# A four-layer graph network on one core: work by half periods, norm and degree roots as powers on GpSimd, and the adjacency scaled once

## The chip, the core and the metric

The kernel runs on one core of a Trainium2 chip. The metric is the device time of one execution in microseconds. The core's engines are TensorE (PE, with its weight loads shown apart as PEld), VectorE (DVE), ScalarE (ACT), GpSimd (POOL) and SyncE (SP, which here only issues DMAs). Each engine works through its own queue in order and waits on semaphores for the others.

## What is computed

There are 64 graphs of 256 nodes with 128 features, and a 256 x 256 adjacency of zeros and ones for each. Four layers follow one another; each adds its result to its input and normalizes the rows (a layernorm without weights):

```python
# layer 0: the largest relu(p_i + q_j + b) over the neighbours j of i
h = jax.nn.relu(p[:, :, None, :] + q[:, None, :, :] + b) * adj[..., None]
x = LN(x + jnp.max(h, axis=2))
# layer 1: sums over neighbours, in both directions, of elu projections, then tanh
upd = jnp.concatenate([adj @ in_rep, node_rep, adj.T @ out_rep], axis=2)
x = LN(x + jnp.tanh(upd @ W_upd.T + b_upd))
# layer 2: two graph convolutions with the normalized adjacency
A_hat = adj + I;  dinv = rsqrt(A_hat.sum(-1));  norm_A = dinv_i * A_hat * dinv_j
h = elu(elu(x @ W0 + b0)); h = elu(norm_A @ (h @ W1) + b1); x = LN(x + norm_A @ (h @ W2) + b2)
# layer 3: a message gelu(LN(m_j + m_i + b1)) for every edge, summed over j, and an update
agg = sum_j adj_ij * gelu(LN(m_j + m_i + b1) * g1 + be1)
x = LN(x + LN(concat(x, agg) @ W2 + b2) * g2 + be2)
```

## The kernel before

A graph's 256 nodes lie as two halves of 128 (h = 0, 1), one row to a partition. Since a node has some 10% to 15% of the others as neighbours, layers 0 and 3 do not form all pairs. Every node's neighbours are counted off into 40 slots; nodes are sorted by degree (the matrix perm), so that slot s is used by a prefix of them, and the prefixes add up to WIDTH = 4800 columns for each half of the neighbours. A 0/1 matrix hot (128 x 2 x 4800) says which neighbour stands in which column, and a product with it spreads the neighbours' features over the columns.

The work on a graph is cut into four generators, which yield now and then:

- `first` (L502): loads x and the adjacency, finds degrees and the sorted order (sign, L551; perm, L560), the ranks, and builds hot on DVE (L629, L635); then, from L645 on, layer 0: products with hot in tiles of 512 columns (L665), corrections for empty slots (L681), maxima on DVE (`fold`, L492), and the norm to x1. It takes 44 calls; the 17th ends with hot.
- `second` (L778, `layer_1`): layer 1, 14 calls. Its first steps are the transposed x1 (L207), the product L223 and the addition L226; its products with the adjacency are L238 and L240.
- `third` (L782, `layer_2`): the degrees' root, the unit matrix added to the adjacency in place (L277), then layer 2 with its two convolutions. Each scales the features by dinv (L293), multiplies them by the adjacency (L296) and the weights (L304), and scales by dinv again (L308). After that come layer 3's projections (c3, dT; L797, L810) and `sums_of` for the first four tiles. It takes 34 calls, of which 23 lead up to dT and 11 are the four `sums_of`.
- `last` (L821): `sums_of` for the remaining six tiles; for each of the ten tiles the product with the fetched scale (L839), Gelu (L841) and the sum over slots (`fold`); then the aggregation (L860) and the update (`update`) with two norms. It takes 34 calls; in its first 18 are five tiles' messages.

`sums_of` (L718) forms the pair sums of a tile of up to 1024 columns (product L728, addition L732), their squares (ACT, L736) and column sums (L743), and sends these through DRAM: line, then vr in a compact form, root and reciprocal there, then scale_line, which `last` fetches spread over all partitions (rs_s, L828). The tile pre that it fills has 7 buffers.

A norm is `layernorm` (L166 on): statistics on DVE, `rs` (L174), a yield, `inverse_root` (Sqrt on ACT, L74, then a reciprocal on DVE, L75), a yield, and the subtraction and scaling on DVE (L180, or L184 and L185). There are five norms to a graph, one root of degrees (dinv), and five roots of vr.

Four graphs are in work at once, one in each stage. `together` runs the generators of one step side by side: it always calls the one that has done the smallest share of its stated number of calls, the oldest stage first on a tie:

```python
STAGES = [(last, 34), (third, 34), (second, 14), (first, 44)]
...
for u in range(1 - len(STAGES), U):
    together(*[
        (n, part(g0 + u + i, ss[u + i])) for i, (part, n) in enumerate(STAGES) if 0 <= u + i < U
    ])
```

So there are 67 steps ("periods") for 64 graphs, of which the first three and the last three are not full. There is no barrier between the periods. The semaphores, the places of the tiles and the final order on each engine come from the tile framework when the kernel is built: it follows the order of the calls and moves some instructions forward (in the trace an addition of `sums_of`, L732, stands between L706 and L707, which `first` issues one after the other).

Of the kernel before, what the change touches and what calls it, by code (L numbers as in the profile page):

```python
# [9 lines left out]
F32 = mybir.dt.float32  # L10
BF16 = mybir.dt.bfloat16
AF = mybir.ActivationFunctionType
ALU = mybir.AluOpType
# [30 lines left out]
def kernel(  # L44
# [24 lines left out]
    minus1 = consts.tile([P, 1], F32, name="minus1")  # L69
    nc.vector.memset(minus1, -1.0)  # L70

    def inverse_root(t):

        nc.scalar.activation(t, t, AF.Sqrt)  # L74
        nc.vector.reciprocal(t, t)  # L75

    def load(src, shape, name):
        t = consts.tile(shape, F32, name=name)
# [78 lines left out]
    class Shared:  # L157
# [45 lines left out]
        def to_features(self, xn, name, bufs=None):  # L203
# [5 lines left out]
            nc.scalar.copy(t, pt[:, :N])  # L209
            return t  # L210

        def node_tile(self, name):
            return self.state.tile([P, H, P], F32, name=name)

# [43 lines left out]
            yield from self.layernorm(x2, y)  # L258
            s["x2"] = x2

        def layer_2(self, s, aT, deg_of):

            work, psum, elu = self.work, self.psum, self.elu
            x2 = s["x2"]
            deg = work.tile([P, H], F32, name="deg")
            deg_of(deg)
            nc.vector.tensor_scalar(deg, deg, 1.0, None, ALU.add)
            pos = work.tile([P, H], F32, name="pos")
            nc.vector.tensor_scalar(pos, deg, 0.0, None, ALU.is_gt)
            dinv = work.tile([P, H], F32, name="dinv")  # L270
            nc.vector.tensor_scalar(dinv, deg, 1e-30, None, ALU.max)
            inverse_root(dinv)
            yield
            nc.vector.tensor_mul(dinv, dinv, pos)
            for h in range(H):
                blk = aT[:, h, h * P:(h + 1) * P]
                nc.vector.tensor_add(blk, blk, ident)  # L277
            yield
            xT = self.to_features(x2, "xT_2", 1)
            yield  # L280
# [8 lines left out]
            yield from elu(hs, hs, twice=True)  # L289
            yield  # L290
            for step in (1, 2):
                for h in range(H):
                    nc.vector.tensor_scalar(hs[:, h], hs[:, h], dinv[:, h:h + 1], None, ALU.mult)  # L293
                pa = psum()
                for h in range(H):
                    nc.tensor.matmul(pa[:, :N], hs[:, h], aT[:, h], start=h == 0, stop=h == H - 1)  # L296
# [14 lines left out]
                if step == 1:  # L311
                    yield from elu(hs, hs)
                yield
# [26 lines left out]

    def together(*gens):

        gens = [[0, n, gen] for n, gen in gens]
        while gens:
            e = min(gens, key=lambda e: e[0] / e[1])
            e[0] += 1
            if next(e[2], gens) is gens:
                gens.remove(e)


# [3 lines left out]
    def sparse(ctx):  # L354
# [147 lines left out]
        def first(g, s):  # L502
# [37 lines left out]
            nc.scalar.activation(diff, diff, AF.Abs, accum_out=fl[:, 0:1])  # L540
            kc = work.tile([P, H, H], F32, name="kc")
            nc.vector.scalar_tensor_tensor(kc, pc, -1.0, down_c, ALU.mult, ALU.subtract)
            dg = state.tile([P, H], F32, name="dg", bufs=3)
            nc.vector.tensor_reduce(dg, pc, AX.X, ALU.add)
            s["dg"] = dg

            more = work.tile([P, H, H], F32, name="more")
            for h in range(H):
# [169 lines left out]
        def sums_of(s, i):  # L718
# [46 lines left out]
                fu[:rows],  # L765
                s["fulls"].rearrange("h w -> (h w)")[first_at:first_at + n].rearrange("(p k) -> p k", k=PIECE),
            )
            inverse_root(vr[:rows])
            nc.vector.tensor_mul(vr[:rows], vr[:rows], fu[:rows])
            out_line = dram.tile([1, GROUP * TILE], F32, name="scale_line")  # L770
            nc.sync.dma_start(out_line[:, :n].rearrange("o (p k) -> (o p) k", k=PIECE), vr[:rows])
# [9 lines left out]

        def third(g, s):  # L782

            dg = s["dg"]

            def deg_of(deg):
                nc.vector.tensor_scalar(deg, dg, 1.0 / N, None, ALU.mult)

            yield from sh.layer_2(s, s["aT"], deg_of)
            yield  # L790
            x3, perm = s["x3"], s["perm"]

# [83 lines left out]


        U = next(u for u in (UNROLL, 8, 4, 2, 1) if B % u == 0)
        STAGES = [(last, 34), (third, 34), (second, 14), (first, 44)]

        def steps(g0):
            ss = [{} for _ in range(U)]
            for u in range(1 - len(STAGES), U):
                together(*[
                    (n, part(g0 + u + i, ss[u + i])) for i, (part, n) in enumerate(STAGES) if 0 <= u + i < U
                ])

        if U == B:
            steps(0)
# [5 lines left out]
    def general(ctx):  # L895
# [82 lines left out]
        def middle(g, s):  # L978
# [7 lines left out]
                nc.scalar.copy(aT[:, hj], pt[:, :N])  # L986
            yield

            def deg_of(deg):
                nc.vector.tensor_reduce(deg, an, AX.X, ALU.add)  # L990

            yield from sh.layer_1(s, an, aT, s["x1"])
            yield
            yield from sh.layer_2(s, aT, deg_of)
            yield

            x3T = sh.to_features(s["x3"], "x3T")
# [80 lines left out]
        def run():  # L1078
            nc.vector.memset(ones3, 1.0)

            with tc.For_i(0, B, U) as g0:
                ss = [{} for _ in range(U)]

                def stage(part, u):
                    return [(1, part(g0 + u, ss[u]))] if u < U else []
# [57 lines left out]
```

## Time and profile before

| what | value |
|---|---|
| median of three runs | 5732.97 us (5730.31 to 5735.6) |
| the profiled execution's own time | 5731.62 us |
| its span, first to last instruction | 5729.7 us |
| instructions | 83531 |
| mean granted TensorE clock | 0.862 of full speed |
| HBM traffic | 345.07 MB read, 14.53 MB written; DMA engines busy about a fifth of the time |
| DVE: pre by rs_s, L839 | 732.9 us in 640 instructions |
| ACT: Gelu, L841 | 594.2 us in 512 instructions and 686.4 us in 535 table loads ahead of it |
| ACT: table loads ahead of Exp, L194 | 283.5 us in 221 |
| POOL | 10 instructions, all in the set-up |

"Busy" is time in which an engine worked on an instruction; the rest of its span it waited. A group in the profile is one line of the kernel on one engine, with the number of its instructions, their busy time, the mean length of one in ns, and the idle time of the engine just before them with what ended it.

### The profile page before, as it was taken

The numbers are of one execution on the slowest core, as the hardware profiler recorded it, in microseconds if no ns is written. First come the engines' busy times: TensorE is split into PE (matmuls) and PEld (weight loads), VectorE is DVE, ScalarE is ACT, GpSimd is POOL, SyncE is SP. The second block draws the span as 40 slices with busy tenths as digits, with TensorE's granted clock in tenths as the row PEclk, the third lists the DMA queues.
The fourth block names the chain that finished last, engine by engine and source line by source line (L and its number), as shares of the span: only waits on it lengthen the run. The fifth ranks groups of instructions, "written<-read, shape, count | busy, mean of one in ns | idle before, by whom it ended". The sixth has DMA issues, their size and how long they took to land.

```text
span 5729.7 us, 83531 instructions
## 1 busy us (share of the span) xinstructions
PE 4529.9 (79%) x27408; PEld 2508.7 (44%) x27408; DVE 4834.4 (84%) x14654; ACT 4275.2 (75%) x6485; POOL 1.9 (0%) x10
## 2 busy tenths in 40 slices
PE   5878878878778778788788788787887887877875
PEld 2444444444444444444444444444444444444443
DVE  6788888888888888888888888888888888888876
ACT  2577777777777777777777777777777777777785
POOL 0000000000000000000000000000000000000000
PEclk8888889889889889888898898898888887888986
DMA  0122222222212221221221222122212212221222
GB/s 22 44 70 63 62 63 72 62 63 66 69 57 70 65 63 63 72 63 62 63 72 62 63 65 70 59 68 65 63 62 72 64 62 63 69 66 60 68 65 74
DMA packets 292813, 365.15 MB, mean 64 GB/s; under 512 B 151952, under 2 KB 210448, under 8 KB 292368
## 3 DMA queue, kind: packets, MB, share of 16 engines
q1 hardware_dynamic: 292368, 359.73, 20.0%
q8 instruction: 217, 3.56, 0.3%
q14 instruction: 228, 1.87, 0.1%
HBM read 345.07 MB, written 14.53 MB: 63 GB/s over the span
## 4 chain that ended last, share of the span: by engine, by line
PE 52%; DVE 29%; ACT 11%; issue 4%; DMA 3%; SPq 0%; DVEq 0%; POOL 0%; ACTq 0%
PE bigp L665 11%; PE bigp L728 8%; DVE pre L839 6%; PE mm L860 5%; DVE lanes L492 4%; PE mm L743 4%; DVE hot L629 4%; DVE pre L732 4%; DVE sums L492 3%; PE bigp L681 3%; DMA rs_s<-scale_line 2%; PE mm L870 2%; PE mm L296 2%; PE mm L699 2%; PE mm L647 2%
## 5 line engine op out<-in xcount | busy, mean ns | idle before, releaser
L665 PE MATMUL bigp<-hot,q 128*128 128x512 fp8e4 (+1 forms) x3840 | 1052.3, 371 | 66.6 <-DVE lanes L492 52.6
L728 PE MATMUL bigp<-hot,c 128*128 128x512 fp8e4 (+1 forms) x3840 | 928.8, 372 | 140.2 <-DVE pre L732 140.2
L732 DVE TENSOR_TENSOR pre<-bigp,dT 128x512 f32<-128x512 f32 (+6 forms) x1664 | 846.3, 530 | 37.8 <-PE bigp L728 33.5
L492 DVE TENSOR_TENSOR lanes<-bigp,lanes 128x512 f32<-128x512 f32 (+6 forms) x1536 | 772.7, 503 | 94.6 <-PE bigp L681 86.9
L839 DVE TENSOR_TENSOR pre<-pre,rs_s 128x1024 f32<-128x1024 f32 (+1 forms) x640 | 732.9, 1150 | 48.6 <-DMA rs_s<-scale_line 48.0
L736 ACT ACTIVATE sq<-pre 128x1024 f32<-128x1024 f32 (+1 forms) x640 | 638.5, 998 | 169.9 <-DVE pre L732 163.9
L841 ACT ACT_TABLE_LOAD x535 | 686.4, 1283 | 9.5
L492 DVE TENSOR_TENSOR sums<-pre,sums 128x1024 f32<-128x1024 f32 (+6 forms) x1024 | 628.8, 614 | 41.2 <-ACT pre L841 40.7
L745 ACT ACTIVATE row<-mm,eps_t 128x256 f32<-128x256 f32 (+1 forms) x640 | 289.6, 453 | 476.9 <-PE mm L743 476.7
L841 ACT ACTIVATE pre<-pre,be,g 128x1024 f32<-128x1024 f32 (+1 forms) x512 | 594.2, 1172 | 57.8 <-DVE pre L839 53.0
L743 PE MATMUL mm<-sq,ones 128*32 128x256 f32 (+1 forms) x5120 | 482.9, 440 | 135.2 <-ACT sq L736 135.2
L74 ACT ACT_TABLE_LOAD x445 | 570.9, 1283 | 7.5
L728 PEld LDWEIGHTS <-c 128*128 128x128 bf16 x3840 | 331.2, 98 | 550.5 <-issue 136.1
L665 PEld LDWEIGHTS <-q 128*128 128x128 bf16 x3840 | 310.8, 97 | 392.6 <-issue 112.0
L296 PE MATMUL mm<-aT,hs 128*128 128x256 f32 x512 | 232.3, 600 | 316.1 <-DVE hs L293 214.8
L629 DVE TENSOR_SCALAR hot<-rank 128x512 fp8e4<-128x512 bf16 (+5 forms) x1536 | 440.5, 348 | 0.0
L681 PEld LDWEIGHTS <-pick 42*128 42x128 bf16 x2944 | 155.8, 95 | 481.5 <-issue 474.2
L296 PEld LDWEIGHTS mm<-aT,hs 128*128 128x128 f32 x512 | 135.6, 293 | 425.8 <-issue 316.1
L860 PE MATMUL mm<-w3u,sums 128*128 128x128 f32 x2048 | 296.7, 289 | 18.4 <-DVE sums L492 16.1
L194 ACT ACT_TABLE_LOAD x221 | 283.5, 1283 | 3.9
L681 PE MATMUL bigp<-lack,pick 42*128 42x36 bf16 (+16 forms) x2944 | 285.7, 187 | 0.0
L860 PEld LDWEIGHTS mm<-w3u,sums 128*128 128x128 f32 x2048 | 254.5, 195 | 37.3 <-issue 17.6
(226 smaller groups left out, 7132.6 us busy)
## 6 DMA issues: line engine op xcount, KB each, us to landing
rs_s<-scale_line SPq DMA_DIRECT2D x512, 512.0 KB
rs_s<-scale_line SPq DMA_DIRECT2D x128, 352.0 KB
an<-in_adj SPq DMA_DIRECT2D x64, 256.0 KB
x<-in_x SPq DMA_DIRECT2D x64, 128.0 KB
line<-row SPq DMA_DIRECT2D x512, 4.0 KB
out<-o SPq DMA_DIRECT2D x64, 128.0 KB
fu<-fulls SPq DMA_DIRECT2D x192, 4.0 KB
vr<-line SPq DMA_DIRECT2D x192, 8.0 KB
```

Source lines behind the costliest of these rows:

```text
L74: nc.scalar.activation(t, t, AF.Sqrt)
L492: nc.vector.tensor_tensor(lanes[:, :k, :w], src[:, i:i + k], lanes[:, :k, :w], op)
L629: nc.vector.tensor_scalar(hot[:, :, at:at + w], rank[:, :, :w], s0 + i + 1.0 - FAR, None, ALU.is_equal, saturate=False)
L665: nc.tensor.matmul(pt[:, :tl], q3[:, i, h], hot[:, h, t0:t0 + tl], start=i == 0, stop=False)
L681: nc.tensor.matmul(o_, l_, r_, start=False, stop=i == len(todo) - 1)
L728: nc.tensor.matmul(pt[:, :bl], c3[:, k, h], hot[:, h, t0 + b:t0 + b + bl], start=k == 0, stop=k == 2)
L732: nc.vector.tensor_add(block(pre[:, b:], n, w, at), block(pt, n, w, at), widen(dT[:, h, :w], n))
L736: nc.scalar.activation(sq[:, :tl], pre[:, :tl], AF.Square)
L743: nc.tensor.matmul(pr[q * Q:(q + 1) * Q, :tl // 4], ones[:, :Q], v4[:, :, q], start=True, stop=True)
L839: nc.vector.tensor_mul(pre[:, :tl], pre[:, :tl], rs[:, :tl])
L841: nc.scalar.activation(msg[:, :tl], pre[:, :tl], AF.Gelu, bias=be3, scale=g3)
L860: nc.tensor.matmul(pt[:, cols], lanes[:, k, cols], w3u[:, 1], start=k == 0, stop=False)
```

## The change

- `inverse_root` becomes one GpSimd instruction, t to the power of -0.5, with a constant tile of -0.5 as second operand. The norms and the degrees use it. The roots of vr in `sums_of` keep Sqrt on ACT and the reciprocal on DVE.
- dinv is made in `first`, right after the degrees (`inverse_root_of`, with the product by pos on GpSimd), and kept in a tile with four buffers; before, `third` made it at the start of layer 2.
- In layer 2 the adjacency, after the unit matrix has been added, is scaled by dinv in place (two DVE instructions of 128 x 256); the scaling of the features ahead of each convolution (L293, four instructions of 128 x 128) goes.
- The stages are cut into parts and a step is half a period: `first` 17 and 27 calls, `second` 14, `third` 23 and 11, `last` 18 and 16. Even half steps hold `first`'s beginning, `second`, `third`'s end and `last`'s end, each for another graph; odd ones hold `first`'s end, `third`'s beginning and `last`'s beginning. There are 2 x 64 + 5 = 133 half steps. `together` stops a generator after the stated number of calls unless the part is the stage's last.

```diff
+    mhalf = consts.tile([P, 16], F32, name="mhalf")
+    nc.vector.memset(mhalf, -0.5)
+
     def inverse_root(t):
 
-        nc.scalar.activation(t, t, AF.Sqrt)
-        nc.vector.reciprocal(t, t)
+        nc.gpsimd.tensor_tensor(t, t, mhalf[:t.shape[0], :t.free_size()], ALU.pow)
...
+        def inverse_root_of(self, deg, bufs):
+
+            nc.vector.tensor_scalar(deg, deg, 1.0, None, ALU.add)
+            pos = self.work.tile([P, H], F32, name="pos")
+            nc.vector.tensor_scalar(pos, deg, 0.0, None, ALU.is_gt)
+            dinv = self.state.tile([P, H], F32, name="dinv", bufs=bufs)
+            nc.vector.tensor_scalar(dinv, deg, 1e-30, None, ALU.max)
+            inverse_root(dinv)
+            nc.gpsimd.tensor_mul(dinv, dinv, pos)
+            return dinv
+
...
-        def layer_2(self, s, aT, deg_of):
+        def layer_2(self, s, aT, dinv_of):
...
-            deg = work.tile([P, H], F32, name="deg")
-            deg_of(deg)
-            nc.vector.tensor_scalar(deg, deg, 1.0, None, ALU.add)
-            pos = work.tile([P, H], F32, name="pos")
-            nc.vector.tensor_scalar(pos, deg, 0.0, None, ALU.is_gt)
-            dinv = work.tile([P, H], F32, name="dinv")
-            nc.vector.tensor_scalar(dinv, deg, 1e-30, None, ALU.max)
-            inverse_root(dinv)
-            yield
-            nc.vector.tensor_mul(dinv, dinv, pos)
+            dinv = dinv_of()
+            yield
             for h in range(H):
                 blk = aT[:, h, h * P:(h + 1) * P]
                 nc.vector.tensor_add(blk, blk, ident)
+            for h in range(H):
+                nc.vector.tensor_scalar(aT[:, h], aT[:, h], dinv[:, h:h + 1], None, ALU.mult)
             yield
...
             for step in (1, 2):
-                for h in range(H):
-                    nc.vector.tensor_scalar(hs[:, h], hs[:, h], dinv[:, h:h + 1], None, ALU.mult)
                 pa = psum()
...
-        gens = [[0, n, gen] for n, gen in gens]
+
+        gens = [[0, n, all_, gen] for n, all_, gen in gens]
         while gens:
             e = min(gens, key=lambda e: e[0] / e[1])
             e[0] += 1
-            if next(e[2], gens) is gens:
+            if next(e[3], gens) is gens or (e[0] == e[1] and not e[2]):
                 gens.remove(e)
...
-            dg = state.tile([P, H], F32, name="dg", bufs=3)
+            dg = work.tile([P, H], F32, name="dg")
             nc.vector.tensor_reduce(dg, pc, AX.X, ALU.add)
-            s["dg"] = dg
+            nc.vector.tensor_scalar(dg, dg, 1.0 / N, None, ALU.mult)
+            s["dinv"] = sh.inverse_root_of(dg, 4)
...
-            inverse_root(vr[:rows])
+            nc.scalar.activation(vr[:rows], vr[:rows], AF.Sqrt)
+            nc.vector.reciprocal(vr[:rows], vr[:rows])
...
-            yield from sh.layer_2(s, s["aT"], deg_of)
+            yield from sh.layer_2(s, s["aT"], lambda: s["dinv"])
...
-        STAGES = [(last, 34), (third, 34), (second, 14), (first, 44)]
+        STAGES = [(first, (17, 27)), (second, (14,)), (third, (23, 11)), (last, (18, 16))]
+        PARTS = [(i, n, n == ns[-1]) for i, (_, ns) in enumerate(STAGES) for n in ns]
 
         def steps(g0):
             ss = [{} for _ in range(U)]
-            for u in range(1 - len(STAGES), U):
-                together(*[
-                    (n, part(g0 + u + i, ss[u + i])) for i, (part, n) in enumerate(STAGES) if 0 <= u + i < U
-                ])
+            gens = {}
+            for t in range(2 * U + len(PARTS) - 2):
+                now = []
+                for u in range(U):
+                    k = t - 2 * u
+                    if 0 <= k < len(PARTS):
+                        i, n, ends = PARTS[k]
+                        if (u, i) not in gens:
+                            gens[u, i] = STAGES[i][0](g0 + u, ss[u])
+                        now.append((n, ends, gens[u, i]))
+                together(*now)
```

A second path for other inputs (`general`), which does not run here, is adapted to the new signatures.

More of the change, by code (lines that the diff above doesn't have):

```diff
@@ L782, in third @@
         def third(g, s):
-            dg = s["dg"]
-            def deg_of(deg):
-                nc.vector.tensor_scalar(deg, dg, 1.0 / N, None, ALU.mult)
-            yield from sh.layer_2(s, s["aT"], deg_of)
+            yield from sh.layer_2(s, s["aT"], lambda: s["dinv"])
             yield
@@ L987, in middle, with dinv_of @@
             yield
-            def deg_of(deg):
+            def dinv_of():
+                deg = work.tile([P, H], F32, name="deg")
                 nc.vector.tensor_reduce(deg, an, AX.X, ALU.add)
+                return sh.inverse_root_of(deg, 1)
             yield from sh.layer_1(s, an, aT, s["x1"])
             yield
-            yield from sh.layer_2(s, aT, deg_of)
+            yield from sh.layer_2(s, aT, dinv_of)
             yield
@@ L1084, in stage @@
                 def stage(part, u):
-                    return [(1, part(g0 + u, ss[u]))] if u < U else []
+                    return [(1, True, part(g0 + u, ss[u]))] if u < U else []
                 together(*stage(first, 0))
```

## The prediction

> **What bounds the kernel now.** I read the page's engine line first, then the windows view over the steady part and over one period cut in two, then the groups by shape for the instructions that go, then the waits. The column order in the windows is length, then busy time and count of PE, PEld, DVE, ACT, POOL, then PEclk.
>
> ```profile
> PE 4529.9 (79%) x27408; PEld 2508.7 (44%) x27408; DVE 4834.4 (84%) x14654; ACT 4275.2 (75%) x6485; POOL 1.9 (0%) x10
> ```
>
> ```profile
> 292.00:5527.00 5235.00, 4213.41 (x25681) 2335.05 (x25682) 4494.55 (x13616) 4019.44 (x6089) 0.00 (x0) 0.87 0.21 65
> ```
>
> ```profile
> 2900.00:2943.00 43.00, 27.02 (x154) 15.63 (x153) 35.45 (x117) 35.11 (x57) 0.00 (x0) 0.80 0.20 62
> 2943.00:2986.60 43.60, 41.70 (x278) 22.89 (x276) 39.09 (x111) 31.12 (x45) 0.00 (x0) 1.00 0.22 69
> ```
>
> ```profile
> L74 ACT ACT_TABLE_LOAD x445 | 570.9, 1283 | 7.5
> ...
> L74 ACT ACTIVATE rs<-rs 128x2 f32<-128x2 f32 x320 | 64.4, 201 | 87.9 <-DVE rs L174 85.8
> ```
>
> ```profile
> PE mm L566 <- DVE perm L560: 245.5, 64, 5.1
> PE mm L296 <- DVE hs L293: 214.8, 67, 8.7
> ...
> DVE io L226 <- PE mm L223: 179.7, 64, 3.1
> ...
> PE mm L207 <- DVE x L180: 107.8, 63, 5.2
> ```
>
> The timeline of tile o has its first finished graph at 291.9 us, then 60 gaps of 87.26 us on average, then the last three of 81.2, 65.1 and 49.5. So the span of 5729.7 is 60 full periods (5235.8) and 493.9 of filling, draining and set-up. In the steady part DVE is busy 4494.6/60 = 74.9 us a period, PE 70.2, ACT 67.0: no engine is full. The two halves differ (2943 is where `first` turns from building hot to its maxima: the copy of q, L497, starts at 2943.1 in the timeline). In the second, PE is busy 41.7 of 43.6 us at full clock and DVE 39.1: it is bound by throughput. In the first PE is busy 27.0 of 43.0 at a clock of 0.80, DVE and ACT 35: it is bound by hand-overs, and the waits name them: PE stands 3.8 us a graph for perm, 3.4 for L293, 1.7 for a layernorm's x, DVE 2.8 for the first product of layer 1.
>
> **What the Trainium skill says.** (1) "ScalarE: Activation LUTs", What ACT_TABLE_LOAD costs: a load takes 1283 ns whatever the set, and a drain of 1380 ns follows. The trace has 1283 exactly; the drain is not seen as idle time (7.5 us before 445 loads). Table sets, there: sqrt, exp and gelu lie in different sets; the trace's loads at L74, L194 and L841 agree. (2) "TensorE: Matmul & The Clock Gate", Part 1: the clock falls when PE has been idle; 0.80 and 1.00 in the two halves agree. (3) "GPSIMD Engine Reference", Key points: it shares its SBUF interfaces with VectorE where DVE has two SBUF inputs, as L839 has (1216 ns each); nothing before shows it, POOL being idle.
>
> **Part by part, per graph.**
>
> Five norms' and one degree's root leave ACT. Activations: 6 x 0.20 = 1.2 us. Loads: the kernel has 1236, 19.3 a graph, 24.8 us. Not all 253 loads that stand at rs and dinv vanish, because Gelu, Exp and the remaining Sqrt of vr still alternate. Walking ACT's timeline, the set needed changes 1296 times; with rs and dinv left out 1105 times, 15% fewer. That is 2.9 loads, 3.7 us. ACT goes from 67.0 to about 62. It lies mostly beside other work, but in the first half ACT is as full as DVE.
>
> DVE loses five reciprocals (48.6/64 = 0.76), dinv's reciprocal and product (0.146 + 0.10), and four L293 (0.95 by the windows of that line). It gains two 128x256 scalings of aT. The form is not there; the nearest are L560 (347 ns each, 284 net of overlap) and L200 (289): 0.57 to 0.69, I take 0.6. The four small degree instructions (0.65) only move to first. Sum: -1.36 us of 74.9. Each L293 pair also stood in the chain before L296: 2 x 0.48 us of latency go; the scaling waits for layer 1's last reader of aT (L238), long done, and is hidden behind the transposes and the first product of layer 2. With that cover gone it costs its 0.6.
>
> POOL gains six powers and one product. No row shows a power. From below, a POOL IOTA on 128x1 takes 133 ns. From above, "GPSIMD Engine Reference", section 3.1, gives 12 cycles for a data-dependent branch per element: 32 elements a core, one after another with ten branches, would be 3.2 us (estimate). I take 1.0. What it replaces: in the period at 2900 the five stretches from the end of L174 to the end of L75 are 0.63, 0.66, 2.50, 3.31 and 2.82 us, 1.98 on average. At 1.0 plus 0.1 of hand-over, the norms of x1, x2, x3 come 1.4 to 2.2 us earlier, the update's two 0.4 later. At 3.2 the three large ones are about level and the update loses 5 us of latency a graph, which lies off the seam beside other work. Queued behind the wait on DVE is whatever follows the norm's last subtraction there; no other work waits on POOL.
>
> Half periods. Calls per part: first 17 + 27, second 14, third 23 + 11, last 18 + 16. Even halves hold first a (to hot), second, third b (four sums_of), last b (the h=1 messages and the update); odd halves first b (the maxima), third a (layer 2), last a. Before, the first half of a period held first a, layer 2 up to its second step, half of second and last a; the second half the rest. From the groups summed by line, PE per part: first a 5.7, first b 23.7, second 6.8, third a 10.5, third b 9.3, last a 12.4, last b 8.5 us (parts overlap, so they add to 77 for 70). Before: 27.4 against 49.5, measured 27.0 and 41.7. After: odd 23.7 + 10.5 + 12.4 = 46.6, scaled by 41.7/49.5 39.3 us; even 30.3, scaled 29.9. The same for DVE, with its -1.36 and the tails of update and x1 that spill over a boundary: odd 39, even 35. The SP queue keeps its order within a stage: line, vr, fu, scale_line and fetches have the same distances in calls, and a call keeps about its length (2.4 to 2.7 us in last). In the even half sums_of(1) needs a pre buffer only 2.4 us after Gelu 5 frees one (13 us before): hidden while PE has other work there, up to 2 us if not.
>
> What is late next: in the odd half layer 2. Its 23 calls had 23/34 of a period, 59 us, and took 66 by the timeline (from the matching start, 2897, to dT at 2963); they now have 43. Its operations alone, added up from their rows, take 24, so it fits, with about 1 us of queueing a step rather than 2. Layer 1's 14 calls go from 87 to 43 us for 16 us of operations. I give back part of the balance for this: odd half 43.0 us (PE and DVE at 91%, the second half now has 96 and 90), even half 41.5 (DVE at 84%, now 82). Period 84.5, against 87.26.
>
> Fill and drain: there are 133 half steps rather than 134, and up to the first output one first b fewer: -20 us, +5 in draining. 493.9 - 15 = 479. Span 479 + 60 x 84.5 = 5549; outside the span lie 5731.6 - 5729.7 = 1.9, so 5551, and the profiled run was 1.4 below the median of the three (5732.97). Forecast **5550 us**, 3.2% faster.
>
> **Rivals.** A, the above, own range 5420 to 5650: periods of 82.3 (both halves at 91% of DVE's 39 and 35, with slack for neither) to 86.1.
>
> B, hidden: the odd half stays as long as the PE-heavy half is now, 43.6, the even half as the first, 43.0, which has no more than ACT's relief; with the longer chain of layer 2 eating the balance the period is 86 to 87.7. For it: PE was not relieved by any removed instruction. Time 5640 to 5745, middle 5700.
>
> C, slower, one mechanism: pace. The odd half has layer 2's chain, the maxima and the sums in one in-order PE queue; each step of layer 2 arrives late and PE stops, as it does 3.4 us a graph at L296 today. If the odd half gets only the DVE share of today's first half, 82%, it takes 39/0.82 = 47.6, the even 35/0.82 = 42.7: period 90.3, 479 + 60 x 90.3 = 5897, with the 1.9 outside the span 5899. It decides when the period passes 87.5, that is when the odd half passes about 45.5 (DVE under 86%). Against it: the even half is relieved of layer 2, and ACT's loads, which delay each step, are fewer.
>
> D, the power is dear, 10 us: three norms 7 us late each, half of it exposed, +11 a period, about 6200. Against it: two elements a row.
>
> That the change doesn't do what it says: all six Sqrt move for certain; only loads may stay, which is in A's low end.
>
> **Chances.** A 0.55, B 0.18, C 0.20, D 0.07. B lies half below 5720. A measurement of this kernel can tell about 0.2% (11 us) from no change. Faster 0.55 + 0.10 = 0.65; same 0.06; slower 0.29, of C, D and the end of B. The range 5420 to 5870 leaves out a low tail of A (0.05), the upper third of C (0.07) and D.
>
> **What would show it.** Right: about 1050 table loads, POOL at 458 instructions with powers near 1 us, DVE busy near 4745, ACT near 3970, the wait of L207 on x down from 107.8, period near 84.5, halves with PE near 39 and 30 us. Wrong: PE's waits at L296, L304 and L285 growing in the odd half (C); DVE waiting for POOL (D); a period of 87 with both waits gone (B).

## The result and the profile after

The changed kernel takes 5814.91 us (median of four runs, 5813.7 to 5815.81) where the kernel before took 5734.28 beside it: a ratio of 1.0142, 95% interval 1.0124 to 1.0159. It is 1.4% slower; the forecast was 3.2% faster. The profiled execution has a span of 5812.7 us. Its timeline of tile o shows the first finished graph at 259.1 us (291.9 before) and then 60 periods of 88.97 us on average (87.26 before). So filling, draining and set-up take 5812.7 - 60 x 88.97 = 474 us, 20 less than before, and the loss of 1.71 us x 60 = 103 us is all in the full periods.

The page's engine line of the changed kernel:

```profile
PE 4588.1 (79%) x27408; PEld 2542.9 (44%) x27408; DVE 4771.0 (82%) x14079; ACT 4088.2 (70%) x6002; POOL 315.7 (5%) x458
```

Work was taken away as intended: DVE is busy 63 us less, ACT 187 us less, on 575 and 483 fewer instructions. But DVE's share fell from 84% to 82%. The span less DVE's busy time is DVE's idle time: 895.3 us before, 1041.6 now. That is +146 of idle against -63 of work.

The windows view, first over the same stretch as before, then over one period, cut where q's product of a new graph stands (2919.8, the odd half's start) and where the graph ahead of it has dT (2973.4). Columns: length, then busy time and count of PE, PEld, DVE, ACT, POOL, then PEclk, DMA share, GB/s.

```profile
292.00:5527.00 5235.00, 4194.21 (x25188) 2327.47 (x25185) 4355.33 (x12842) 3773.57 (x5535) 290.38 (x413) 0.91 0.21 64
2919.80:2973.40 53.60, 45.04 (x246) 20.71 (x246) 41.79 (x115) 38.13 (x51) 2.50 (x4) 0.87 0.21 63
2973.40:3010.40 37.00, 28.69 (x191) 18.37 (x189) 29.79 (x91) 25.31 (x42) 2.50 (x3) 0.86 0.15 47
```

The halves have indeed been redealt: PE, busy 27 and 42 us of the two halves before, now has 29 and 45. But neither half is full any more. (This is one period, of 90.6 us.) Over 42 periods of the timeline the two stretches last 51.0 and 38.0 us on average, DVE is busy 43.6 us of the first (86%) and 30.4 of the second (80%), PE 42.3 (83%) and 29.1 (76%). Before, PE was busy for 96% of its heavy half. (The two marks are not the exact ends of the half steps, which the engines do not reach together.)

What PE waits for, in the changed kernel (total us, times, longest):

```profile
PE mm L573 <- DVE perm L567: 306.6, 63, 7.6
PE mm L750 <- ACT sq L743: 187.4, 116, 11.5
PE bigp L672 <- DVE pre L739: 126.5, 125, 4.6
PE mm L863 <- DVE sums L498: 102.9, 44, 14.8
PE mm L813 <- ACT dn L806: 91.3, 64, 2.4
PE mm L698 <- DVE total_m L695: 89.2, 79, 3.7
...
PE mm L209 <- DVE x L182: 42.0, 60, 4.9
PE mm L292 <- ACT xT L211: 38.8, 41, 1.8
...
PE mm L301 <- DVE hs L203: 13.6, 23, 4.2
...
PE mm L309 <- ACT agg L304: 8.4, 22, 1.1
```

L573, L209 and L301 are L566, L207 and L296 of before. The waits that the norms' roots and the features' scaling stood in are gone or smaller: 214.8 became 13.6, 107.8 became 42.0. The wait for perm grew from 245.5 to 306.6, that for the squares from 135.2 to 187.4, and those for the pair sums (at L672 and L735) from 141.3 to 163.5. Three waits that were some 16 us each before are 89 to 103 now: for the last folding ahead of the aggregation (L863), for dn (L813) and for total_m (L698). Layer 2's first product (L292), which did not wait before, waits 38.8.

PE's own time has changed too: the same 27408 products keep it busy 58 us longer (4588.1 against 4529.9). The largest part is the aggregation, two groups of products a graph, each behind the last folding of a half of the neighbours. First before, then now:

```profile
L860 PE MATMUL mm<-w3u,sums 128*128 128x128 f32 x2048 | 296.7, 289 | 18.4 <-DVE sums L492 16.1
```

```profile
L863 PE MATMUL mm<-w3u,sums 128*128 128x128 f32 x2048 | 434.9, 375 | 102.9 <-DVE sums L498 102.9
```

By the clock records of the two traces, these products ran at a mean granted clock (weighted by their length) of 0.98 of full speed before and of 0.67 now. Layer 2's convolutions (L296, now L301) went the other way, from 600 ns at 0.59 to 399 ns at 0.96.

What DVE waits for, first in the kernel before, then in the changed one:

```profile
...
DVE rest L498 <- ACT q L497: 93.4, 54, 3.4
DVE lanes L492 <- PE bigp L681: 86.9, 172, 2.0
DVE y L330 <- PE mm L870: 72.1, 64, 4.9
...
DVE sums L492 <- ACT pre L841: 40.7, 67, 2.3
...
DVE rs L75 <- ACT rs L74: 6.6, 36, 0.5
```

```profile
DVE y L335 <- PE mm L873: 160.8, 63, 5.3
DVE sums L498 <- ACT pre L844: 127.9, 59, 2.7
DVE nd L246 <- PE mm L243: 110.7, 63, 3.4
DVE m L713 <- ACT m L712: 82.6, 43, 4.5
...
DVE x L182 <- POOL rs L77: 58.9, 129, 1.2
```

These are the larger shares of the 146 us: the update's y +89 (its product stands behind the aggregation), the folding of sums after Gelu +87, m +52, the pair sums +47 (33.5 to 80.4), and the waits on POOL (58.9 here, 77 in all) against 6.6 on ACT before. Against them the wait of q's remainder for ACT (93.4) is gone, and layer 1's first additions (io and nd together 185 before, 118 now) and the maxima (87 to 18) gave some back.

### The profile page after: what moved, and what is told of

Read it like the earlier page. It is cut to its first block, busy times and chain, and to the rows that moved or that the text cites. A ratio compares the mean times of both kernels' runs of the same rounds, so it can differ in the third digit from the quotient of the medians.

```text
span 5812.7 us, 82666 instructions
## 1 busy us (share of the span) xinstructions
PE 4588.1 (79%) x27408; PEld 2542.9 (44%) x27408; DVE 4771.0 (82%) x14079; ACT 4088.2 (70%) x6002; POOL 315.7 (5%) x458
## 4 chain that ended last, share of the span: by engine, by line
PE 45%; DVE 24%; ACT 23%; issue 5%; POOL 1%; DMA 1%; SPq 0%; DVEq 0%; ACTq 0%; POOLq 0%
PE bigp L672 10%; PE mm L863 7%; ACT L844 4%; PE mm L750 4%; PE bigp L735 3%; DVE pre L739 3%; ACT L775 3%; DVE hot L636 3%; ACT pre L844 3%; DVE pre L842 3%; DVE sums L498 3%; PE mm L873 3%; PE bigp L688 2%; ACT sq L743 2%; DVE lanes L498 2%
## 5 line engine op out<-in xcount | busy, mean ns | idle before, releaser
L672 PE MATMUL bigp<-hot,q 128*128 128x512 fp8e4 (+1 forms) x3840 | 1121.0, 388 | 231.5 <-DVE pre L739 126.5
L735 PE MATMUL bigp<-hot,c 128*128 128x512 fp8e4 (+1 forms) x3840 | 934.0, 374 | 59.9 <-DVE pre L739 37.0
L739 DVE TENSOR_TENSOR pre<-bigp,dT 128x512 f32<-128x512 f32 (+6 forms) x1664 | 843.1, 530 | 83.1 <-PE bigp L735 80.4
L498 DVE TENSOR_TENSOR lanes<-bigp,lanes 128x512 f32<-128x512 f32 (+6 forms) x1536 | 770.2, 501 | 23.6 <-PE bigp L688 17.7
L842 DVE TENSOR_TENSOR pre<-pre,rs_s 128x1024 f32<-128x1024 f32 (+1 forms) x640 | 731.0, 1148 | 24.0 <-DMA rs_s<-scale_line 23.5
L498 DVE TENSOR_TENSOR sums<-pre,sums 128x1024 f32<-128x1024 f32 (+6 forms) x1024 | 625.5, 611 | 134.2 <-ACT pre L844 127.9
L750 PE MATMUL mm<-sq,ones 128*32 128x256 f32 (+1 forms) x5120 | 449.3, 390 | 187.8 <-ACT sq L743 187.4
L844 ACT ACT_TABLE_LOAD x444 | 569.7, 1283 | 7.8
L672 PEld LDWEIGHTS <-q 128*128 128x128 bf16 x3840 | 318.3, 100 | 541.0 <-issue 244.7
L735 PEld LDWEIGHTS <-c 128*128 128x128 bf16 x3840 | 335.9, 99 | 469.8 <-issue 171.5
L863 PE MATMUL mm<-w3u,sums 128*128 128x128 f32 x2048 | 434.9, 375 | 102.9 <-DVE sums L498 102.9
L77 POOL TENSOR_TENSOR rs<-rs,mhalf 128x2 f32<-128x2 f32 x320 | 223.0, 704 | 5024.0 <-DVE rs L176 4778.2
L775 ACT ACT_TABLE_LOAD x318 | 408.0, 1283 | 79.0 <-DMA vr<-line 73.9
L863 PEld LDWEIGHTS mm<-w3u,sums 128*128 128x128 f32 x2048 | 376.0, 273 | 155.1 <-DVE sums L498 107.7
L196 ACT ACT_TABLE_LOAD x251 | 322.0, 1283 | 4.4
L573 PE MATMUL mm<-perm,nz 128*128 128x256 bf16 x256 | 80.3, 357 | 306.6 <-DVE perm L567 306.6
```

What stands on the lines that cost most here:

```text
L498: nc.vector.tensor_tensor(lanes[:, :k, :w], src[:, i:i + k], lanes[:, :k, :w], op)
L672: nc.tensor.matmul(pt[:, :tl], q3[:, i, h], hot[:, h, t0:t0 + tl], start=i == 0, stop=False)
L735: nc.tensor.matmul(pt[:, :bl], c3[:, k, h], hot[:, h, t0 + b:t0 + b + bl], start=k == 0, stop=k == 2)
L739: nc.vector.tensor_add(block(pre[:, b:], n, w, at), block(pt, n, w, at), widen(dT[:, h, :w], n))
L750: nc.tensor.matmul(pr[q * Q:(q + 1) * Q, :tl // 4], ones[:, :Q], v4[:, :, q], start=True, stop=True)
L775: nc.scalar.activation(vr[:rows], vr[:rows], AF.Sqrt)
```

## The experiments

All times are medians; each ratio is to the kernel before, run beside it. For orientation, the table of all kernels that are built from the change's parts. "Roots" is the norms' and degrees' root as a power on GpSimd, "scaled" the adjacency scaled once; the degree's root stays in `third` here.

| period | neither | roots | scaled | both |
|---|---|---|---|---|
| whole, as before | 5728 | 5686 | 5696 | 5623 |
| halves, `third` cut 23/11 | 5824 | 5711 | not run | 5812 |
| halves, `third` cut 18/16 | 5802 | 5395 | 5611 | 5582 |

### The parts, one at a time

Half periods alone: the kernel before with the new stages and the new `together`, nothing else.

```diff
-        STAGES = [(last, 34), (third, 34), (second, 14), (first, 44)]
+        STAGES = [(first, (17, 27)), (second, (14,)), (third, (23, 11)), (last, (18, 16))]
```

> The kernel before with the half periods alone; roots and scaling as before. Theory P (pace: the half periods cost, the other two parts gain): 5820 to 5930 us, period 89 to 92. Theory R (roots: the power on GpSimd costs, the half periods gain a little): 5650 to 5740. Theory O (no part costs by itself; the framework's order of the instructions changes with any edit and the effects do not add up): anything, but halves plus whole-period version would not add up to the change's +81 within 30 us.

Measured: 5824.15 us, ratio 1.0167 (1.015 to 1.0184).

Roots alone, with whole periods:

```diff
-        nc.scalar.activation(t, t, AF.Sqrt)
-        nc.vector.reciprocal(t, t)
+        nc.gpsimd.tensor_tensor(t, t, mhalf[:t.shape[0], :t.free_size()], ALU.pow)
```

> The kernel before with the five norms' and the degrees' roots as powers on GpSimd, nothing else. Theory P: 5620 to 5700 us, with some 150 table loads fewer. Theory R: 5760 to 5830, DVE or PE waiting for L77-like powers. Theory O: no firm sign.

Measured: 5686.05 us, ratio 0.9928 (0.9912 to 0.9945).

Scaling alone, with whole periods:

```diff
+            for h in range(H):
+                nc.vector.tensor_scalar(aT[:, h], aT[:, h], dinv[:, h:h + 1], None, ALU.mult)
...
-                for h in range(H):
-                    nc.vector.tensor_scalar(hs[:, h], hs[:, h], dinv[:, h:h + 1], None, ALU.mult)
```

> The kernel before with the adjacency scaled once and L293 gone, nothing else. P and R: 5690 to 5725 us (DVE 0.4 us a graph less, and twice 0.5 us less latency ahead of the convolutions). Theory O: no firm sign.

Measured: 5695.5 us, ratio 0.9936 (0.9919 to 0.9952).

The changed kernel with whole periods (roots, scaling, and the degree's root made in `first`): the diff of the stages above, reversed.

> The changed kernel with whole periods (roots as powers, dinv made in the first stage, adjacency scaled once, but the old cutting of stages). Theory P: 5580 to 5680 us. Theory R: 5760 to 5830. Theory O: differs from the sum of roots alone and scaling alone by more than 30 us.

Measured: 5774.59 us, ratio 1.0069 (1.0046 to 1.0091).

Roots and scaling each gain 34 to 44 us. The half periods lose 94 us on their own. And f4_whole is slower than before although it holds both gains, so something else in it costs: the only other edit is the place of the degree's root (with its product by pos, now on GpSimd, and the four buffers of dinv).

Roots and scaling together, degree's root in `third` as before (the two diffs above):

> The kernel before with the roots as powers and the adjacency scaled once, dinv made at the start of layer 2 as before (whole periods). The two alone gave -44 and -34 us, with dinv moved to the first stage the three together +45. Theory M (the move of dinv costs some 120 us): 5640 to 5670 us. Theory I (roots and scaling spoil each other): 5750 to 5800.

Measured: 5623.44 us, ratio 0.9818 (0.9802 to 0.9834). In whole periods the two edits together gain 103 us, more than the 78 of the two alone, and moving the degree's root into `first` then costs 5774.6 - 5623.4 = 151 us.

Roots, scaling and half periods, degree's root in `third`:

> The changed kernel with dinv made at the start of layer 2 again (half periods, roots, scaling). Theory M, if the costs add: the changed kernel less some 100 us, 5700 to 5740, that is the half periods' +94 less 78. Theory I: 5790 to 5840, as the changed kernel.

Measured: 5812.18 us, ratio 1.0151 (1.0134 to 1.0168), the same as the whole change (1.0142). In half periods the root's place costs nothing; the half periods themselves cost 5812 - 5623 = 189 us.

### The degree's root in first

The kernel before with only dinv made in `first`, behind the degrees (root still on ACT and DVE):

```diff
+            nc.vector.tensor_scalar(dg, dg, 1.0 / N, None, ALU.mult)
+            s["dinv"] = sh.inverse_root_of(dg, 4)
...
-            yield from sh.layer_2(s, s["aT"], deg_of)
+            yield from sh.layer_2(s, s["aT"], lambda: s["dinv"])
```

> The kernel before with dinv made in the first stage right after the degrees, its root still on ACT and DVE, nothing else (whole periods). Theory M: 5800 to 5860 us. Theory I: 5720 to 5745, no change.

Measured: 5831.79 us, ratio 1.0187 (1.017 to 1.0204): seven small instructions in another place cost 105 us. Their own time is not it: DVE executes the same 14654 instructions as before. The traces show that the order changes with the place. Take f4_whole, where the move costs 151 us against g1_roots_scale. Counted from `nz`, the first DVE instruction of a new graph, the degree's own instructions on DVE now stand at 39.6 to 40.1 us of a period, just ahead of a wait of DVE. Besides them and two small ones of vr, DVE's order over a period is the same but for two instructions: `diff` (L516, 0.69 us) stands at 0.3 us of the period where it was at 16.2 in g1_roots_scale, and a folding of sums (1.22 us) at 6.6 us where it was at 0.5. From there all is 1.3 us later, and DVE then waits longer for the update's product. The wait in g1_roots_scale and in f4_whole:

```profile
DVE y L332 <- PE mm L873: 91.2, 64, 4.4
```

```profile
DVE y L335 <- PE mm L872: 233.3, 64, 4.1
```

This wait alone grew by 142 us; others moved against each other (layer 1's io -98, the pair sums +69, the fetched scales +38).

But the place of `diff` does not explain g2_dinv_first, where the move costs 105 us. There `diff` stands at 14.9 us, and in the kernel before it stands at 0.3: the other way round. The order differs in many places, the wait at y is shorter (46.5 us against 72.1), and the wait that grew most is that for the products of the maxima, from 86.9 us (shown above) to:

```profile
DVE lanes L495 <- PE bigp L685: 171.6, 204, 3.7
```

Two more runs ask about the cause. First, the degree's root later in `first`, when hot is complete:

```diff
             s["hot"] = hot
+            nc.vector.tensor_scalar(dg, dg, 1.0 / N, None, ALU.mult)
+            s["dinv"] = sh.inverse_root_of(dg, 4)
```

> The kernel before with the degree's root made in first, as in the run that did so and took 5832 us, but after the hot rows of the graph are complete rather than right behind the degree. Root still on ScalarE and the reciprocal on VectorE. Theory place (the root stands in the middle of the sign chain and holds it up): here it stands behind it, and the time is that of the kernel before, 5720 to 5750 us. Theory order (what costs is that the four small instructions are gone from the start of layer 2 in third, so that other work moves up there): the time stays near 5830 us, 5800 to 5860.

Measured: 5804.17 us, ratio 1.0133 (1.0111 to 1.0154). So it is not that the root stands among the signs. `diff` stands at 14.9 us here too. Second, four DVE instructions of the degree's size, whose result nobody uses, at the start of layer 2 in `third`, in f4_whole:

```diff
+            more = work.tile([P, H], F32, name="again")
+            nc.vector.tensor_scalar(more, s["dinv"], 1.0 / N, None, ALU.mult)
+            nc.vector.tensor_scalar(more, more, 1.0, None, ALU.add)
+            nc.vector.tensor_scalar(more, more, 0.0, None, ALU.is_gt)
+            nc.vector.tensor_scalar(more, more, 1e-30, None, ALU.max)
             yield from sh.layer_2(s, s["aT"], lambda: s["dinv"])
```

> The changed kernel with whole periods (5775 us when the degree's root is made in first, 5623 us when it is made in third), and four small VectorE instructions without use put back at the start of layer 2 in third, where the degree's were. More work than the run of 5775 us. Theory order (the missing instructions let other work move up, and what that pushes back costs): the time falls to 5610 to 5680 us. Theory place (it is the root's new place in first that costs): 5770 to 5800 us.

Measured: 5781.22 us, ratio 1.0088 (1.0061 to 1.0116), and `diff` stays at 0.3 us. The time is that of the theory of the place. But in the trace these four instructions stand at 41.3 to 43.9 us of the period, not at 18 us, where the degree's own instructions were in g1_roots_scale. They did not fill the gap, so the run does not decide whether the missing instructions let other work move up. Shown is that the root's place in `first` costs 76 to 151 us in whole periods, each time with another order on DVE, and that the waits in which the time is lost are not the same in f4_whole and g2_dinv_first. Which neighbours cost, and why the framework orders them so, stays open.

### Where third is cut

The same instructions in another order: the changed kernel with `third` cut after 18, 16 or 20 of its 34 calls instead of 23, that is (18, 16), (16, 18) and (20, 14).

```diff
-        STAGES = [(first, (17, 27)), (second, (14,)), (third, (23, 11)), (last, (18, 16))]
+        STAGES = [(first, (17, 27)), (second, (14,)), (third, (18, 16)), (last, (18, 16))]
```

> The changed kernel with the third stage cut after 18 of its calls instead of 23: the odd half step has layer 2 up to its norm only, the even one the projections and the four sums. Theory P (the odd half is too full: 51 us from the product of q to dT, against 38 for the rest): 5700 to 5780 us, the two halves nearer to each other. If the halves cost because there are two hand-overs a period, wherever they are cut: 5800 to 5850.

Measured: 5582.89 us, ratio 0.9752 (0.9736 to 0.9768).

> The changed kernel with third cut (16, 18) rather than (23, 11). Theory balance: the time is a smooth curve over where third is cut; at 18/16 it is 5583 us, at 23/11 5815, and at 16/18 the even half becomes lighter still on the other side, so the time lies near 18/16's, 5560 to 5660 us. Theory ordering: each cut gives another order of the engines' instructions and the time jumps without regard to the balance; then anything from 5550 to 5850 us, and the sequence 16, 18, 20, 23 is not smooth.

Measured: 5673.74 us, ratio 0.9911 (0.989 to 0.9932).

> The changed kernel with third cut (20, 14). Theory balance: two fifths of the way from the 18/16 cut (5583 us) to the 23/11 cut (5815 us), so 5640 to 5720 us. Theory ordering: no relation to the two neighbours, 5550 to 5850 us.

Measured: 5701.15 us, ratio 0.9948 (0.9929 to 0.9967).

With 5815 at 23 calls this looks like a valley: 5674, 5583, 5701, 5815, as the theory of balance had it (met at 20, just missed at 16). It is lowest where the calls of the odd and the even half are equal (27 + 18 + 18 = 63 against 17 + 14 + 16 + 16 = 63). If the count were the cause, `first` cut (22, 22) with `third` left at (23, 11) would do as well, since it also gives 63 and 63.

```diff
-        STAGES = [(first, (17, 27)), (second, (14,)), (third, (23, 11)), (last, (18, 16))]
+        STAGES = [(first, (22, 22)), (second, (14,)), (third, (23, 11)), (last, (18, 16))]
```

> The changed kernel with first cut (22, 22) rather than (17, 27), third left at (23, 11). Counted in steps of the generators, the odd half (second part of first, first parts of third and last) holds 27 + 23 + 18 = 68 of 126 in the changed kernel and 63 with third cut 18/16; with this cut it also holds 63. Theory balance: the time falls as with third's cut 18/16, to 5550 to 5650 us. Theory place (it is the place of third's cut, not the balance): 5780 to 5850 us.

Measured: 7046.09 us, ratio 1.2323 (1.2287 to 1.236). Neither theory had this. Its engine line:

```profile
PE 4917.9 (70%) x27408; PEld 2684.6 (38%) x27408; DVE 4874.9 (70%) x14079; ACT 3812.9 (54%) x5754; POOL 417.6 (6%) x458
```

DVE has 2% more work and is idle for 2127 us; PE waits 577.1 us for perm and 417.5 us at the first convolution of layer 2. Balance in calls is not the rule. That it is what a cut puts side by side, and in which order, is what remains; no run isolates it.

What the cut at 18 changed for DVE:

```profile
DVE y L335 <- PE mm L873: 107.1, 64, 4.3
DVE sums L498 <- ACT pre L844: 98.1, 125, 2.1
...
DVE io L239 <- PE mm L236: 61.8, 63, 1.6
...
DVE nd L246 <- PE mm L243: 48.6, 62, 2.3
```

Against 160.8, 127.9, 7.1 and 110.7 in the changed kernel; all its idle time is 793 us instead of 1042, with 4786 us of work instead of 4771. So the gain of 232 us is less idle time; the work did not shrink.

On PE, the aggregation is back to a wait of 15.7 us and 306.8 us of work (296 ns each, mean granted clock 0.95), together 215 us less than in the changed kernel. Its length follows the cut in all kernels that were measured: 359 to 379 ns at clocks of 0.66 to 0.71 wherever `third` is cut at 23 or 20, and 287 to 308 ns at clocks of 0.87 to 0.99 with whole periods or `third` cut at 18 or 16. So it goes with the cut and accounts for much of what PE loses between 18 and 23, but it is not shown to set the time: with the cut at 20 it waits 316.6 us and works 409.1, more than at 23, and that kernel is still faster by 114 us.

### Half periods at the better cut, edit by edit

Half periods alone, cut 18/16, against the kernel before:

```diff
-        STAGES = [(last, 34), (third, 34), (second, 14), (first, 44)]
+        STAGES = [(first, (17, 27)), (second, (14,)), (third, (18, 16)), (last, (18, 16))]
```

> The kernel before with the half periods alone, cut 18/16 in third instead of 23/11: roots on ScalarE, adjacency unscaled, degree's root in third. With the 23/11 cut this was 5824 us, 1.017 of the kernel before. Theory balance (the fuller odd half set the loss): the loss goes, 5640 to 5740 us. Theory that half periods themselves cost (fewer graphs side by side in the odd or even half, whatever the cut): 5780 to 5830 us.

Measured: 5801.6 us, ratio 1.0127 (1.0108 to 1.0145). The better cut alone does not save the half periods.

The same with the roots on GpSimd (the diff of the roots alone on top):

> Half periods cut 18/16 with the roots on GpSimd, adjacency not scaled, degree's root in third. Half periods at this cut alone took 5802 us. Theory ScalarE (in the odd half its 83 per cent is what holds TensorE's squares up, and the roots relieve it): most of the way to 5583 us, 5600 to 5700 us. Theory sum (the roots give what they give with whole periods, 44 us): 5740 to 5780 us.

Measured: 5395.05 us, ratio 0.9418 (0.9399 to 0.9438), far below both expectations. It is the fastest kernel found, 5.8% under the kernel before. Its engine line, and DVE's waits:

```profile
PE 4356.0 (81%) x27408; PEld 2426.3 (45%) x27408; DVE 4785.5 (89%) x14271; ACT 4099.5 (76%) x5999; POOL 281.5 (5%) x394
```

```profile
DVE x L182 <- POOL rs L77: 62.3, 131, 0.9
DVE y L332 <- PE mm L874: 55.8, 64, 5.3
DVE nd L235 <- PE mm L232: 44.2, 62, 2.3
DVE sums L495 <- ACT pre L845: 40.9, 65, 2.1
DVE io L228 <- PE mm L225: 40.5, 64, 2.0
```

DVE is idle for 611 us, the least of all. It does no less than the changed kernel does (4785.5 against 4771.0 us).

Half periods at 18/16 with the scaling (its diff on top) and without the roots:

> Half periods cut 18/16, adjacency scaled once, roots left on ScalarE, degree's root in third. Half periods at this cut alone took 5802 us, with the roots moved 5395, with both edits 5582. Theory sums (what the scaling does is the same with either root, +187 us): 5970 to 6010 us. Theory order (each of these kernels lands on one of several ways in which the graphs stand against each other, and no sum holds): anywhere from 5580 to 5850 us, likeliest near 5800.

Measured: 5611.37 us, ratio 0.98 (0.9784 to 0.9816). So the scaling gains 190 us here where the roots are on ACT.

Half periods at 18/16 with both diffs on top, degree's root in `third`:

> The changed kernel with third cut 18/16 and the degree's root made in third, as before: half periods, roots on GpSimd and the adjacency scaled once. With the 23/11 cut the root's place made no difference (5812 and 5815 us). Theory balance: none here either, 5560 to 5610 us. Theory order: the place decides again, 5620 to 5800 us.

Measured: 5581.73 us, ratio 0.9746 (0.9726 to 0.9765): the same as with the root in `first` (0.9752), as at the cut of 23. The scaling, which gained 190 us without the roots, loses 187 beside them.

The roots at the change's own cut of 23/11, without the scaling (the diffs of half periods alone and roots alone):

> Half periods at the change's own cut (23/11), roots on GpSimd, adjacency not scaled, degree's root in third. Theory cut (the 23/11 cut holds the graphs up whatever else is in the period: half periods alone 5824 us, with both other edits 5812): 5780 to 5820 us. Theory scaling (the scaling costs some 190 us in half periods, as at 18/16): 5600 to 5680 us.

Measured: 5710.76 us, ratio 0.9973 (0.9961 to 0.9985), between the two expectations. So no part has a price of its own here: at 23/11 the half periods alone lose 94 us, the roots on top of them gain 113, and the scaling on top of both loses 101.

DVE's work lies between 4771 and 4875 us in all 19 changed kernels, and their spans between 5396 and 7001 us. So the difference lies in how long DVE stands idle, 611 to 2127 us. This tells where the time went, not why: PE's busy time on the same 27408 products ranges from 4356 us (i4_hr_third18) to 4918 (i1_first22) as well. That the edits act through the order that they lead to fits all runs; it is argued, since every edit changes order and waits together.

## Why the prediction was wrong

The prediction overrated the removed work somewhat, and failed at one step: "odd half 43.0 us (PE and DVE at 91%, the second half now has 96 and 90), even half 41.5 (DVE at 84%, now 82)". It took the busy shares of the halves as given and let the half periods bring part of the gain. In place of 43.0 and 41.5 us the stretches took 51.0 and 38.0, at 86% and 80% of DVE; the half periods alone lose 94 us (f1_halves), and cost 189 on top of roots and scaling, which by themselves bring 103 of the 184 us that were forecast. Point by point:

- **ACT.** Forecast about 1050 table loads and 3970 us busy; measured 1137 and 4088. The 87 loads more, at 1283 ns, are 112 of the 118 us. The size of the cut was underrated (roots alone go from 1236 to 954, not to 1050), and what the half periods do to the loads was not seen: alone they raise them to 1360, of which 121 of the 124 new ones stand ahead of the elus (L194, L198) and the tanh of layer 1 (L254).
- **DVE.** Forecast 1.36 us a graph less (4745 us), measured 0.99 (4771). With whole periods, the roots alone took off 0.53 (forecast 0.91) and the scaling alone 0.23 (forecast 0.35). The adjacency's scaling took 40.1 us, 0.63 a graph (forecast 0.6).
- **The power.** Forecast 1.0 us with 0.13 to 3.2 as bounds; measured 0.70 for the norms' and 0.97 for the degrees'. From the end of rs to the finished root it takes 0.85 us instead of 1.96. Half periods alone raised this to 2.51. Rival D is excluded. The POOL lines, by shape:

```profile
L77 POOL TENSOR_TENSOR rs<-rs,mhalf 128x2 f32<-128x2 f32 x320 | 223.0, 704 | 5024.0 <-DVE rs L176 4778.2 <-DVE mv L174 242.5 <-DVE vr L776 3.1
...
L77 POOL TENSOR_TENSOR dinv<-dinv,mhalf 128x2 f32<-128x2 f32 x64 | 62.3, 974 | 443.6 <-DVE dinv L220 443.6
...
L222 POOL TENSOR_TENSOR dinv<-dinv,pos 128x2 f32<-128x2 f32 x64 | 28.5, 445 | 5.0
```

- **Roots and scaling with whole periods.** They were not forecast apart, but the direction of both was right: 0.9928 and 0.9936, 0.9818 together.
- **The degree's root in `first`** was forecast at 0.65 us of work that only moves. The work is that small; the new order that came with it costs 105 us (g2_dinv_first) and 151 (f4_whole against g1_roots_scale) in whole periods, nothing in half periods. No rival had it.
- **Filling and draining.** Forecast 479 us, measured 474.
- **The halves.** This is the term that failed: 60 periods of 88.97 instead of 84.5, 268 us, which is the whole miss (5814.9 against 5550, 265). The forecast took the share of time that DVE and PE reach in a half from halves of the kernel before, and moved the work between them. (Its best case for A is added up wrong: 39/0.91 and 35/0.91 make 81.3 us, not 82.3. The miss lies on the other side.) The work by measured stretches was 43.6 and 30.4 us for DVE (forecast 39 and 35). At the forecast shares of 91% and 84% this would still give 47.9 + 36.2 = 84.1 us. The shares were 86% and 80%, 51.0 + 38.0. In this reckoning the unequal halves cost nothing in the sum, and the lower shares cost all of it. A half did not keep its busy share when the work in it was dealt anew; why the shares fell is not isolated.
- **Rival C** ("pace", 5899 us, period 90.3, chance 0.20) came nearest in size and had the low share, but largely not the place. Of its three signs, PE's waits at L296 and L304 shrank (L301 and L309 now, 13.6 and 8.4 us) and only that at L285 grew (L292 now, none to 38.8). PE's and DVE's larger waits are at perm, the squares, the aggregation, y, nd and the sums. In one thing C was nearer than A: layer 2 did not fit the half. Between the marks that the prediction used (the unit matrix's addition and dT) it takes 58.9 us on average, against 66.7 before and the 43 that A gave it.
- **Rival B** (hidden) is excluded: it allowed a period of 86 to 87.7 us and an odd half of 43.6.

What is not settled: which pair of neighbours in the order makes 5395 us of one combination and 5582 of the next. Between i4_hr_third18 and i3_hrs_third18, about three quarters of DVE's instructions keep their order over a period; the others differ mainly where layer 2 meets the maxima and at the start of a new graph. The period of the one measures 82.18 us, that of the other 85.26. No run isolates a single exchange there.

## What to carry to other kernels

Where several engines are each 70% to 85% busy and none is full, the removed work says little of the time: at most 1.3% of the busiest engine's work was removed here, and the time moved by -6% to +23%. Do not carry a busy share from one schedule over to another; give such a change a range as wide as the reorderings that it brings (here 4% over the cuts of `third`, and 21% for one cut of `first`). Measure each edit with each schedule, because the best set of edits is not the sum of those that gain alone, and keep a version that leaves one out: without the scaling, with the degree's root left in `third` and with another cut, the change's idea gives 0.9418 instead of 1.0142.

## What the runs showed of the hardware

GpSimd's power of two elements a partition takes 689 ns at the least, and up to 1597. The view of tile dinv in the changed kernel (minimum, median, maximum in ns):

```profile
L77 POOL TENSOR_TENSOR dinv<-dinv,mhalf x64: 689/691/1597, 39.5 to 5558.4; 128x2 f32<-128x2 f32 x64
L222 POOL TENSOR_TENSOR dinv<-dinv,pos x64: 196/221/933, 40.3 to 5559.1; 128x2 f32<-128x2 f32 x64
```

What DVE does meanwhile sorts them. 20 of the 64 powers run beside a folding of two SBUF tiles of 128x1024 (L498) for 1.05 us and take 1594 to 1597 ns, ending some 0.55 us after the folding. 21 overlap such a folding only in their last 0.26 us and take 689 to 691, as the 23 without a folding do (690 to 708). The small products that follow go the same way: 927 to 933 ns in the 21 that run beside a folding for 0.87 us, 196 to 222 in the others. This agrees with "GPSIMD Engine Reference", Key points, in the Trainium skill, which says that GpSimd shares its SBUF interfaces with VectorE and contends with its instructions that have two SBUF inputs. In this trace GpSimd alone pays: the 41 foldings of this shape beside GpSimd take 1216 ns, the other 215 take 1213. The product of pre by rs_s (L842), which also reads two SBUF tiles, never ran beside GpSimd here.

A shorter latency can still be waited for longer. The root is ready 1.1 us earlier than before, yet DVE now waits 58.9 us for it at the norms' x (L182) alone, where the reciprocal at L75 waited 6.6. Before, 2.02 us of other work stood on DVE between rs and the instruction that needs the root; now 1.00 us stands there, and for 24 of the 320 norms none.
